# Mirroring the block triangle of a two-layer graph kernel, and storing turned dilation decisions for the second layer

## The chip, the cores and the metric

The kernel runs on one core of a Trainium2 chip. A core has five engines that run at the same time, each through its own queue of instructions in order: TensorE (PE in the profile, its weight loads PEld), VectorE (DVE), ScalarE (ACT), GpSimd (POOL) and SyncE (SP). SP and POOL also issue DMA transfers, which 16 DMA engines carry out. The metric is the device time of one execution in microseconds (us), the median of several runs.

## The reference

The input is 16 graphs of N = 1024 nodes with 128 features, and a dense weighted adjacency matrix for each graph whose pattern of non-zeros is symmetric while its values are not.

```python
# layer 0: three convolutions, each
h = h @ W + b
nh = h / max(norm(h), EPS)
ew = adj * (nh @ nh.T)          # the cosine matrix is symmetric, adj is not
h = ew @ h                      # relu between them
x = x + h

# layer 1
keep = dilate(adj > 0)          # row by row, each removal clears its mirror too
adj_d = adj * keep
for i in (1, 2, 3):
    agg = (adj_d @ x) / clip(adj_d.sum(-1), 1)
    out = agg @ Wr + x @ Wx + b
    h_i = batchnorm(relu(out / max(norm(out), NORM_EPS)))
x = x + concat(h_1, h_2, h_3) @ Wl + bl
```

The dilation is sequential: row n counts its neighbours, and if there are more than ten it removes those whose running rank divides evenly by half the count; what row n removes is also removed from column n, before the next row is looked at.

## The kernel before, in words

The adjacency of a graph is 8 x 8 blocks of 128 x 128. The kernel works on block rows q of the upper triangle with the diagonal: row q holds the blocks (q, q) to (q, 7), and beside them their mirror images from below the diagonal, so that one tile of `2 * (8 - q) - 1` blocks carries both. Row 0 is the longest, row 7 the shortest.

Layer 0 (class `Batch`) goes through the rows in the order of `SEQ`, a long one and a short one in turn. For a row, `products` makes the cosine blocks once by matmul and multiplies them into both halves of the tile (the diagonal block by an instruction of its own); `turn` transposes the mirror half on PE; `sums` and `sums_back` add up the result. `adjT_tile` loads the adjacency of a row, transposes the blocks of one half and stores them to DRAM (`adjT_d`) for the second layer.

The dilation runs at the same time, spread between the steps of layer 0. It is cut into 16 pieces: block row k (0 to 7) by half of the graphs (8 each). At the start of a piece, `loads` fetches for each graph the adjacency rows (`an`), and the decisions that earlier rows made on these columns: the tile `pk` (named `kl`, two buffers), loaded from `keep_d` by a transposing DMA on SP's queue (L810). `rounds` solves the sequential rule inside the diagonal block, and `scans` writes the row's decisions `kp` as 0 or 1 in half precision to `keep_d`, 128 rows of 1024, through POOL's queue (L989).

The instructions of layer 0 and the dilation are put in order by the class `Plan` in the kernel itself: it simulates the five queues with prices of its own, a landing time of 3.5 us for a DMA among them, and fixes the order on every engine. The second layer after it is ordered by the framework's scheduler, which moves ready instructions ahead of those that still wait.

In the first part of the second layer ("stage First" below) the kernel takes one graph after the other. `fetch` loads all decisions of a graph (`kb`, eight loads of 128 x 1024, L407) one graph ahead. For each row q, `load_row` loads the transposed half from `adjT_d` (L396) and the plain half from the input (L398); `masked` turns the decisions of the blocks (q, q) to (7, q) on PE into PSUM (L1416), multiplies them with those of row q on DVE (L1418, an edge stays only if neither side removed it), and applies the product to both halves of the adjacency (L1424 and L1428); `turn` transposes the masked mirror half (L1441), copies it back on ACT (L1442) and stores both halves to `adT_d` (L1443 and L1445) for the later convolutions; `First.add` adds up the aggregation (L1199) two rows behind, `weigh` divides by the degree (L1221 to L1225) and `norms` normalises four blocks (L1113 on ACT, L366, L369, L1115 and L1132 on DVE). The next convolution of the graph before (`onward`, L1253 and L1261) and its transposes (`keep`, L1138) are put between the rows. The tiles of a row are used by every second graph, so that the load of a row waits until `onward` has read the tile for the last time.

Of the kernel before, what the change touches and what calls it, by code (L numbers as in the profile page):

```python
# [9 lines left out]
F32 = mybir.dt.float32  # L10
# [9 lines left out]
P = 128  # L20
# [18 lines left out]
SEQ = (0, 7, 1, 6, 2, 5, 3, 4)  # L39
# [220 lines left out]
def tile_adj_preln_d2(  # L260
# [49 lines left out]
    def base(q):  # L310


        return q * 2 * NCH - q * q
# [3 lines left out]
    adT_d = [dram.tile([NCH, P, N], F32, tag=f"adT{b}", name=f"adT{b}") for b in range(B)]  # L317
    sum_d = [[dram.tile([P, N], F32, tag=f"sum{l}_{b}", name=f"sum{l}_{b}") for b in range(B)] for l in (1, 2)]
# [64 lines left out]
    EARLY = (0, 1)  # L383
    early, kept = {}, {}

    def row_of(b, q):

        pool, tag = kept["early" if q in EARLY else "rows"], f"aT{q}"
        if b % 2:
            pool, tag = kept["rows"], f"aTo{q}"  # L390
        return pool.tile([P, 2 * (NCH - q) - 1, P], F32, tag=tag, name=f"aT{q}_{b}")

    def load_row(b, q):
        row = NCH - q
        aT = row_of(b, q)
        nc.sync.dma_start(aT[:, :row, :].rearrange("p c q -> p (c q)"), adjT_d[b][q][:, q * P :])  # L396
        if row > 1:
            nc.sync.dma_start(  # L398
                aT[:, row:, :].rearrange("p c q -> p (c q)"), adj[b][q * P : (q + 1) * P, (q + 1) * P :]
            )  # L400
        return aT

    def fetch(b):

        kb = kept["k"].tile([P, NCH, N], F16, tag="kb", bufs=2, name=f"kb_{b}")
        for c in range(NCH):
            nc.sync.dma_start(kb[:, c, :], keep_d[b][c * P : (c + 1) * P, :])  # L407
# [5 lines left out]
    with ExitStack() as actx:  # L413
# [42 lines left out]
        def adj_piece(b, q):  # L456
            Nat[b, q] = nat = poold.tile([P, NCH, P], F32, tag="nat", bufs=4, name=f"nat_{b}_{q}")
            nc.sync.dma_start(
                nat[:, : NCH - q, :], adj[b][q * P :, q * P : (q + 1) * P].rearrange("(c p) q -> p c q", p=P)
            )  # L460

        def adjT_tile(b, q):

            place, nat, row = adj_place(b, q), Nat.pop((b, q)), NCH - q
            if row > 1:
                nc.sync.dma_start(
                    place[:, row:, :].rearrange("p c q -> p (c q)"), adj[b][q * P : (q + 1) * P, (q + 1) * P :]
                )
            for c in range(0, row, CPH):
# [4 lines left out]
                nc.scalar.activation(place[:, c : c + n, :], pt[:, :n, :], AF.Copy)  # L474
            nc.gpsimd.dma_start(adjT_d[b][q][:, q * P :], place[:, :row, :].rearrange("p c q -> p (c q)"))  # L475

        class Batch:
# [65 lines left out]
            def products(self, s):  # L543
# [5 lines left out]
                row = NCH - q  # L549

                most = max(NCH - SEQ[s % 4], NCH - SEQ[s % 4 + 4])
                ew = pool1.tile([P, 2 * most - 1, P], F32, tag=f"ew{s % 4}", name=f"ew_{nm}")
                place = adj_place(self.b, q)
                both = [t[:, 1 : 2 * row - 1, :].rearrange("p (t c) q -> p t c q", t=2) for t in (ew, place)] if row > 1 else None
                for c in range(0, row, CPH):
# [5 lines left out]
                        rhs=self.nhT[:, (q + c) * P : (q + c + n) * P],  # L561
# [3 lines left out]
                    own = c == 0  # L565
                    if own:
                        nc.vector.tensor_tensor(ew[:, 0, :], pg[:, 0, :], place[:, 0, :], ALU.mult)  # L567
                    if n > own:
                        off = slice(c + own - 1, c + n - 1)
                        nc.vector.tensor_tensor(  # L570
                            both[0][:, :, off, :],
                            pg[:, own:n, :].unsqueeze(1).to_broadcast([P, 2, n - own, P]),
# [5 lines left out]
            def turn(self, s, ew):  # L578

                q = SEQ[s]  # L580
                row = NCH - q
                for c in range(1, row, CPH):
                    n = min(CPH, row - c)
                    pt = ps_t.tile([P, CPH, P], F32, tag="gt", name=f"gt_{self.b}_{self.l}_{q}_{c}")
                    at = row + c - 1
                    for i in range(n):
                        nc.tensor.transpose(pt[:, i, :], ew[:, at + i, :], ident)  # L587
                    nc.scalar.activation(ew[:, at : at + n, :], pt[:, :n, :], AF.Copy)  # L588

            def sums(self, s, ew):  # L590
# [4 lines left out]
                for h in range(q // CPH, NHALF):  # L595
                    c = max(q, h * CPH)
                    n = (h + 1) * CPH - c
# [3 lines left out]
                        rhs=ew[:, c - q : c - q + n, :].rearrange("p c q -> p (c q)"),  # L601
# [4 lines left out]
            def sums_back(self, s, ew):  # L606

                q = SEQ[s]

                closes = all(c // CPH > q // CPH for c in SEQ[s + 1 :])  # L610
                for n in range(1, NCH - q):
                    nc.tensor.matmul(  # L612
                        self.po[:, q * P : (q + 1) * P],
                        lhsT=self.hS[:, q + n, :],
                        rhs=ew[:, NCH - 1 - q + n, :],
                        start=False,
                        stop=closes and n == NCH - 1 - q,
# [35 lines left out]
        def layer0():  # L653
# [29 lines left out]
            for i, now in enumerate(order + [None]):  # L683
# [5 lines left out]
                for s in range(NCH if now else LAG):  # L689
                    q = SEQ[s]  # L690
                    if now:
                        behind.append((now, s, *now.products(s)))
                        yield (NCH - q) * COLS
                    late = None
                    if len(behind) > LAG or not now:
                        late, s_, ew = behind.pop(0)
                        late.sums(s_, ew)
                        yield (NCH - SEQ[s_]) * COLS
                    if s > 0 and now or s == 0 and i:
                        b_, *of = behind[-2 if now else -1]  # L700
                        if now or s == 0:
                            b_.turn(*of)
                            yield (NCH - 1 - SEQ[of[0]]) * TURN
                    if late:
                        late.sums_back(s_, ew)
                        yield (NCH - 1 - SEQ[s_]) * COLS
                    if not now:
                        continue
                    while pieces_at < len(pieces) and pieces[pieces_at][0] == (i, s):
# [4 lines left out]
                        yield (NCH - pieces[pieces_at - 1][1][1]) * TURN  # L714
# [63 lines left out]
        def dilate(k, half, exact):  # L778
# [20 lines left out]
            def loads():  # L799
                for i in range(BH):  # L800
# [7 lines left out]
                    if k:  # L808
# [3 lines left out]
                        )  # L812
                        nc.vector.scalar_tensor_tensor(
# [272 lines left out]
    with ExitStack() as bctx:  # L1086
# [79 lines left out]
        class First:  # L1166
# [29 lines left out]
            def add(self, q, aT):  # L1196

                def one(c, blk, source):
# [4 lines left out]
                        start=source == 0 and c % self.ga == 0,  # L1203
                        stop=c == q and source == NCH - 1 and (c == NCH - 1 or c % self.ga == self.ga - 1),
                    )

                row = NCH - q
                for c in range(q, NCH):
                    one(c, c - q, q)
                for n in range(1, row):  # L1210
                    one(q, row + n - 1, q + n)
# [459 lines left out]
```

## Time and profile before

| | |
|---|---|
| time, median of 3 runs | 2672.81 us (2667.66 to 2675.88) |
| the profiled execution | 2669.1 us, of which 2667.4 us lie between its first and last instruction |
| PE busy | 2588.9 us, 97% |
| DVE, ACT, POOL busy | 1787.9 us, 1470.4 us, 688.5 us |
| granted TensorE clock, mean | 0.993 |
| layer 0 with the dilation | 0 to about 1410 us, the rest of layer 0 to about 1530 us |
| stage First | about 1530 to 2160 us, 38.5 us for a graph in its steady part |
| later convolutions | to the end |

In the lines of the profile, a row of a group names the line, the engine, the operation, the tiles written and read, the shapes and the count; then the busy time of the group, the mean length of one instruction, and how long the engine sat idle before. Matmuls overlap: the length of one is its latency, and the distance between two starts is what it takes from PE. Single-precision matmuls (not transposes) go through PE in two passes, and each pass is a row of the trace.

### The profile page before, as it was taken

Reading aid. Unit: us, or ns where it says so; the run is one execution under the profiler, and the core shown is the slowest. Engines: PE = TensorE matmul, PEld = TensorE weight load, DVE = VectorE, ACT = ScalarE, POOL = GpSimd, SP = SyncE. Lnnn points to the kernel's source line nnn. Section 1 sums busy time; section 2 is a strip of 40 time slices with the busy share of each in tenths; the row PEclk is TensorE's granted clock in tenths of the full one; section 3 lists DMA queues with packets and bytes.
Section 4 is the critical chain, followed back from the end, with each engine's and each line's share of the span. In section 5 each row is a group of like instructions: output and inputs, shape, how many; then the busy total and the mean of one; then the engine's idle time right before and its main releaser. Section 6 shows DMA issues by size and latency. Waiting matters only on the chain. (4 is left out here: it accounts for less than half of the span.)

```text
span 2667.4 us, 48644 instructions
## 1 busy us (share of the span) xinstructions
PE 2588.9 (97%) x16761; PEld 1992.4 (75%) x16761; DVE 1787.9 (67%) x4799; ACT 1470.4 (55%) x4209; POOL 688.5 (26%) x1141
## 2 busy tenths in 40 slices
PE   8999999999999999999999999999999999999978
PEld 6777777777777777777776789889889865655678
DVE  3767778777877789788784465555546545565565
ACT  6868687577666676575563333323333335555565
POOL 4122222122221222222220132333323322222460
PEclk9999999999999999999999999999999999999999
DMA  9457386285565587584642099999999979999427
GB/s 291 142 177 225 102 253 199 64 254 176 139 211 136 166 254 169 149 258 121 177 152 101 17 307 293 319 278 291 317 276 287 278 213 377 347 348 331 155 80 222
DMA packets 400705, 576.70 MB, mean 216 GB/s; under 512 B 87809, under 2 KB 277249, under 8 KB 400449
## 3 DMA queue, kind: packets, MB, share of 16 engines
q1 hardware_dynamic: 348416, 391.72, 48.0%
q0 software_dynamic: 52032, 181.78, 22.4%
q8 instruction: 135, 2.21, 0.3%
q14 instruction: 122, 0.99, 0.1%
HBM read 369.89 MB, written 188.81 MB: 209 GB/s over the span
## 5 line engine op out<-in xcount | busy, mean ns | idle before, releaser
L558 PE MATMUL pg<-nhT 128*128 128x512 f32 (+3 forms) x1152 | 445.9, 490 | 11.1 <-DVE ew L570 7.1
L598 PE MATMUL po<-ew,hS 128*128 128x512 f32 (+3 forms) x1152 | 445.2, 491 | 6.1 <-PEq L1071 3.6
L570 DVE TENSOR_TENSOR ew<-pg,adjA 128x768 f32<-128x768 f32 (+3 forms) x528 | 430.0, 824 | 1.0 <-PE pg L558 0.8
L612 PEld LDWEIGHTS po<-ew,hS 128*128 128x128 f32 x2688 | 338.7, 192 | 39.2 <-issue 38.3
L612 PE MATMUL po<-ew,hS 128*128 128x128 f32 x2688 | 366.5, 276 | 0.0
L588 ACT ACTIVATE ew<-gt 128x512 f32<-128x512 f32 (+1 forms) x480 | 209.3, 467 | 234.3 <-PE gt L587 229.0
L535 POOL TENSOR_TENSOR hS<-hN,rn 128x128 f32<-128x128 f32 x384 | 169.3, 474 | 481.3 <-DVE rn L369 360.2
L598 PEld LDWEIGHTS po<-ew,hS 128*128 128x128 f32 x1152 | 193.8, 191 | 94.9 <-issue 62.9
L567 DVE TENSOR_TENSOR ew<-pg,adjA 128x128 f32<-128x128 f32 x384 | 108.3, 282 | 226.3 <-PE pg L558 151.2
L558 PEld LDWEIGHTS pg<-nhT 128*128 128x128 f32 x1152 | 187.2, 191 | 94.9 <-issue 65.9
L1199 PE MATMUL agg<-hw,aT 128*128 128x129 f32 x2048 | 257.8, 276 | 0.0
L1199 PEld LDWEIGHTS agg<-hw,aT 128*128 128x128 f32 x2048 | 241.2, 191 | 0.0
L587 PEld LDWEIGHTS gt<-ident,ew 128*128 128x128 f32 x1344 | 165.7, 141 | 96.9 <-issue 74.0
L1536 PE MATMUL sumb<-aT,o 128*128 128x512 f32 x512 | 225.5, 593 | 1.8 <-ACT o L1130 1.8
L587 PE MATMUL gt<-ident,ew 128*128 128x128 f32 x1344 | 208.7, 274 | 1.8 <-DVE ew L570 1.4
L1442 ACT ACTIVATE aT<-pta 128x512 f32<-128x512 f32 (+3 forms) x160 | 71.2, 467 | 205.9 <-PE pta L1441 194.1
L1536 PEld LDWEIGHTS sumb<-aT,o 128*128 128x128 f32 x512 | 94.6, 190 | 109.2 <-issue 99.2
L532 ACT ACTIVATE hS<-hN 128x128 f32<-128x128 f32 x384 | 114.6, 302 | 77.6 <-DVE hN L516 62.7
L475 POOL DMA_DIRECT2D adjT<-adjA x128 | 70.6, 552 | 335.6 <-ACT adjA L474 295.8
L1418 DVE TENSOR_TENSOR both<-pkb,kb 128x1024 f16<-128x1024 f16 (+7 forms) x128 | 57.6, 450 | 147.7 <-PE pkb L1416 128.9
L1253 PE MATMUL next<-aT,o 128*128 128x512 f32 (+3 forms) x384 | 151.1, 497 | 0.0
L974 ACT ACTIVATE kp<-rank,fin 128x1024 f16<-128x1024 uint8 x128 | 146.7, 1150 | 6.7 <-DMA keep<-kp 5.1
(213 smaller groups left out, 5054.5 us busy)
## 6 DMA issues: line engine op xcount, KB each, us to landing
an<-in_adj_dram SPq DMA_DIRECT2D x128, 512.0 KB, 5.0
aT<-adT SPq DMA_DIRECT2D x128, 512.0 KB, 8.9
keep<-kp POOLq DMA_DIRECT2D x128, 256.0 KB
kb<-keep SPq DMA_DIRECT2D x128, 256.0 KB, 6.5
sum<-sum POOLq DMA_DIRECT2D x64, 256.0 KB
A<-sum SPq DMA_DIRECT2D x32, 512.0 KB, 4.1
xb<-in_x_dram SPq DMA_DIRECT2D x31, 512.0 KB, 4.6
adT<-aT POOLq DMA_DIRECT2D x32, 448.0 KB
```

The costliest lines, as they stand in the source:

```text
L532: nc.scalar.activation(hS[:, c, :], self.hN[:, c, :], AF.Square, accum_out=ss[:, c : c + 1])
L535: nc.gpsimd.tensor_tensor(hS[:, c, :], self.hN[:, c, :], self.rn[:, c : c + 1].to_broadcast([P, D]), ALU.mult)
L558: nc.tensor.matmul(pg[:, :n, :].rearrange("p c q -> p (c q)"), lhsT=self.nhT[:, q * P : (q + 1) * P], rhs=self.nhT[:, (q + c) * P : (q + c ...
L570: nc.vector.tensor_tensor(both[0][:, :, off, :], pg[:, own:n, :].unsqueeze(1).to_broadcast([P, 2, n - own, P]), both[1][:, :, off, :], ALU ...
L587: nc.tensor.transpose(pt[:, i, :], ew[:, at + i, :], ident)
L588: nc.scalar.activation(ew[:, at : at + n, :], pt[:, :n, :], AF.Copy)
L598: nc.tensor.matmul(self.po[:, c * P : (c + n) * P], lhsT=self.hS[:, q, :], rhs=ew[:, c - q : c - q + n, :].rearrange("p c q -> p (c q)"), ...
L612: nc.tensor.matmul(self.po[:, q * P : (q + 1) * P], lhsT=self.hS[:, q + n, :], rhs=ew[:, NCH - 1 - q + n, :], start=False, stop=closes and ...
L974: nc.scalar.activation(kp, rank if exact else rank.bitcast(U8).rearrange("p (c l) -> p c l", l=2)[:, :, i % 2], AF.Abs, bias=shift[:, i : ...
L1199: nc.tensor.matmul(self.place(c), lhsT=aT[:, blk, :], rhs=self.hw[:, source, :], start=source == 0 and c % self.ga == 0, stop=c == q and s ...
L1253: nc.tensor.matmul(self.bank[:, (c - h * CPH) * P :], lhsT=self.o[:, q, :], rhs=aT[:, c - q : hi - q, :].rearrange("p c q -> p (c q)"), st ...
L1536: nc.tensor.matmul(banks[h], lhsT=now.o[:, q, :], rhs=aT[:, h * HALF : (h + 1) * HALF], start=q == 0, stop=q == NCH - 1,)
```

## The change

The triangle is mirrored: a row q now holds the blocks (q, 0) to (q, q), so that row 7 is the longest, and all loops over rows, sources and halves run the other way round. In a tile the plain half now comes first and the turned half with the diagonal block behind it. In `products` the diagonal block lies at the end of a row, not at its beginning.

In the dilation, the decisions that a transposing DMA has loaded for block row k (the blocks above the diagonal, turned) are now also stored, through POOL's queue, to a new DRAM tensor `keepT_d`. In the second layer `fetch` loads for each row q the plain decisions of the blocks (q, 0) to (q, q) and the turned ones of the blocks (0, q) to (q-1, q), by 15 loads in place of 8, the bytes being the same. `masked` turns only the diagonal block on PE, and multiplies the others from the two loaded halves on DVE.

```diff
-SEQ = (0, 7, 1, 6, 2, 5, 3, 4)
+SEQ = (7, 0, 6, 1, 5, 2, 4, 3)
...
     def base(q):
-        return q * 2 * NCH - q * q
+        return q * q
...
+    keepT_d = [dram.tile([N, N], F16, tag=f"keepT{b}", name=f"keepT{b}") for b in range(B)]
...
-    EARLY = (0, 1)
+    EARLY = (7, 6)
...
     def load_row(b, q):
-        row = NCH - q
         aT = row_of(b, q)
-        nc.sync.dma_start(aT[:, :row, :].rearrange("p c q -> p (c q)"), adjT_d[b][q][:, q * P :])
-        if row > 1:
-            nc.sync.dma_start(
-                aT[:, row:, :].rearrange("p c q -> p (c q)"), adj[b][q * P : (q + 1) * P, (q + 1) * P :]
-            )
+        nc.sync.dma_start(aT[:, q:, :].rearrange("p c q -> p (c q)"), adjT_d[b][q][:, : (q + 1) * P])
+        if q:
+            nc.sync.dma_start(aT[:, :q, :].rearrange("p c q -> p (c q)"), adj[b][q * P : (q + 1) * P, : q * P])
         return aT

     def fetch(b):
-        kb = kept["k"].tile([P, NCH, N], F16, tag="kb", bufs=2, name=f"kb_{b}")
-        for c in range(NCH):
-            nc.sync.dma_start(kb[:, c, :], keep_d[b][c * P : (c + 1) * P, :])
+        kb = kept["k"].tile([P, base(NCH), P], F16, tag="kb", bufs=2, name=f"kb_{b}")
+        for q in reversed(range(NCH)):
+            rows = slice(q * P, (q + 1) * P)
+            for of, lo, n in ((keep_d, base(q) + q, q + 1), (keepT_d, base(q), q)):
+                if n:
+                    nc.sync.dma_start(kb[:, lo : lo + n, :].rearrange("p c q -> p (c q)"), of[b][rows, : n * P])
...
             def products(self, s):
...
-                    own = c == 0
+                    own = c + n == row
                     if own:
-                        nc.vector.tensor_tensor(ew[:, 0, :], pg[:, 0, :], place[:, 0, :], ALU.mult)
+                        nc.vector.tensor_tensor(ew[:, 2 * q, :], pg[:, n - 1, :], place[:, 2 * q, :], ALU.mult)
                     if n > own:
-                        off = slice(c + own - 1, c + n - 1)
+                        off = slice(c, c + n - own)
...
                         nc.sync.dma_start(
                             pk[:, :k, :].rearrange("p j q -> p (j q)"), keep_d[b][: k * P, cols], transpose=True
                         )
+                        nc.gpsimd.dma_start(keepT_d[b][cols, : k * P], pk[:, :k, :].rearrange("p j q -> p (j q)"))
...
             def masked(b, q, kb):
-                row = NCH - q
...
-                pk = ps_t.tile([P, NCH, P], F16, tag="pk", name=f"pkb_{b}_{q}")
-                for c in range(row):
-                    nc.tensor.transpose(pk[:, c, :], kb[:, q + c, q * P : (q + 1) * P], ident16)
+                k0 = base(q)
+                own = kb[:, k0 + 2 * q, :]
+                pk = ps_t.tile([P, P], F16, tag="pk", name=f"pkb_{b}_{q}")
+                nc.tensor.transpose(pk, own, ident16)
                 both = poolk.tile([P, NCH, P], F16, tag="both", bufs=2, name=f"both_{b}_{q}")
-                nc.vector.tensor_tensor(
-                    both[:, :row, :],
-                    pk[:, :row, :],
-                    kb[:, q, q * P :].rearrange("p (c q) -> p c q", q=P),
-                    ALU.mult,
-                )
-                nc.vector.scalar_tensor_tensor(
-                    aT[:, :row, :], aT[:, :row, :], 0.0, both[:, :row, :], ALU.max, ALU.mult
-                )
-                if row > 1:
-                    nc.vector.scalar_tensor_tensor(
-                        aT[:, row:, :], aT[:, row:, :], 0.0, both[:, 1:row, :], ALU.max, ALU.mult
-                    )
+                nc.vector.tensor_tensor(both[:, q, :], pk, own, ALU.mult)
+                if q:
+                    nc.vector.tensor_tensor(
+                        both[:, :q, :], kb[:, k0 : k0 + q, :], kb[:, k0 + q : k0 + 2 * q, :], ALU.mult
+                    )
+                    nc.vector.scalar_tensor_tensor(aT[:, :q, :], aT[:, :q, :], 0.0, both[:, :q, :], ALU.max, ALU.mult)
+                nc.vector.scalar_tensor_tensor(
+                    aT[:, q:, :], aT[:, q:, :], 0.0, both[:, : q + 1, :], ALU.max, ALU.mult
+                )
                 return aT
...
                 if len(behind) > LAG1: ...
-                if q == CPH + 1:
-                    s.norms(0)
-                if q == NCH - 1:
-                    s.norms(1)
+                if q == CPH - 1:
+                    s.norms(1)
+                if q == 0:
+                    s.norms(0)
...
-                for q in range(NCH):
+                for r in range(NCH):
+                    q = NCH - 1 - r
...
-                        was.onward(0, 0, 1)
+                        was.onward(1, 7, 6)
```

In `weigh`, banks of three block columns are closed from the end: the columns 6 and 7 first, then 3 to 5, then 0 to 2. `adjT_tile`, `turn`, `sums`, `sums_back`, `First.add` and `onward` change only in the direction of their indices.

## The prediction

> **What bounds the kernel now.** I read the table by stages first: stretches of 100 us, with the busy time of PE (count), PEld, DVE, ACT and POOL, the granted clock, the DMA share and GB/s. The first row lies in layer 0, the second in stage First.
>
> ```profile
> 600.00:700.00 100.00, 97.70 (x626) 71.96 (x625) 83.66 (x213) 66.82 (x175) 20.66 (x39) 1.00 0.41 123
> ...
> 1700.00:1800.00 100.00, 99.84 (x763) 87.73 (x763) 51.92 (x150) 29.47 (x96) 29.45 (x47) 1.00 0.99 283
> ```
>
> PE is full in both, at the full granted clock. In First the DMA share of 0.99 looks like a second bound, so I read the DMA next: one graph of First (it begins at 1800.03 with its first mask transpose) in stretches of 2 us, and the waits of SP's queue in First (who, for whom, us in total, times, longest).
>
> ```profile
> 1800.00:1802.00 2.00, 1.92 (x13) 1.58 (x12) 0.00 (x0) 1.21 (x3) 0.54 (x1) 1.00 1.06 402
> ...
> 1810.00:1812.00 2.00, 2.00 (x20) 1.96 (x19) 2.00 (x7) 1.09 (x5) 2.00 (x3) 1.00 1.05 397
> ...
> 1818.00:1820.00 2.00, 2.00 (x21) 2.00 (x20) 1.26 (x5) 0.00 (x0) 1.30 (x2) 1.00 0.96 24
> ```
>
> ```profile
> SPq L396 <- PE next L1253: 224.2, 12, 20.5
> SPq L398 <- DMA hN<-h: 17.3, 13, 1.4
> ```
>
> The loads are a burst: at about 400 GB/s for some 18 us, then 24 GB/s with SP waiting up to 20.5 us per graph until PE has read the old row tiles. The transfers thus follow PE; DMA is not the bound over a graph, but it is full in the first half. There the DVE is full too (2.00 of 2.00 at 1810). Last I read the lines that the change takes away, and how they lie on PE.
>
> ```profile
> L1416 PE MATMUL pkb<-ident,kb 128*128 128x128 f16 x576 | 55.5, 219 | 0.0
> ```
>
> ```profile
> 1805.22 0.55 PE L1416 MATMUL pkb<-ident,kb 128*128 128x128 f16 x7
> 1805.61 1.08 PE L1253 MATMUL next<-aT,o 128*128 128x512 f32 x2
> ...
> 1808.68 0.50 PE L1416 MATMUL pkb<-ident,kb 128*128 128x128 f16 x6
> 1809.02 1.35 PE L1199 MATMUL agg<-hw,aT 128*128 128x129 f32 x10
> 1810.21 0.88 PE L1441 MATMUL pta<-ident,aT 128*128 128x128 f32 x6
> ```
>
> One transpose is 219 ns long, but seven in a row let the next matmul start after 1805.61 - 1805.22 = 0.39 us, six after 0.34: each takes 0.056 us from PE. The group's 55.5 us (0.096 us each) counts tails that overlap the next work.
>
> **The change, part by part.** The sum is made against the profiled execution, 2669.1 us, 3.7 us below the median of 2672.8.
>
> *Removed on PE.* Of 576 mask transposes the 16 x 8 = 128 diagonal ones stay, 448 go: 448 x 0.056 = 25.1 us, or 28 x 0.056 = 1.57 us for a graph, in a stage where PE has no gap that would swallow it. The Trainium skill would price them higher: "TensorE: Matmul & The Clock Gate", Part 4: PE-mode transpose, gives about 275 ns for a 16-bit one inside a kernel; 448 of these would be an estimated 123 us. The spacing in the trace decides, since the transposes here are issued back to back.
>
> *DVE in First.* L1418 (616 ns for 7 blocks, 225 for one) becomes one multiply of the diagonal block and one of the others, from SBUF. No row shows this with both inputs from loaded tiles except L944, 688 ns for 1024 elements against 692 for L1418 of that size, so I take the same rate: 0.2 us more a row. DVE is at 52%, and the multiply of the other blocks no longer waits for PE.
>
> *What is late next.* The order of the changed program tells. Times from the graph's first mask transpose (1800.03 now). PE: `pw` starts at 0.46 as now and takes 3.46, two aggregations (four passes of 0.112) and a mask transpose end at 4.43, seven `pta` at 0.109 at 5.20, an aggregation and a mask transpose at 5.48, six `pta` at 6.14, then 30 passes, a mask transpose and 22 passes: PE reaches the `pta` of the third row (q = 5) at 12.0. DVE must have masked that row. Its steps (lengths less 0.08 us, by which the timeline shows them to overlap): the fourth bias add ends at 4.99 (ACT hands it over at 4.6, as now); diagonal mask 0.15, masks of row 5 0.38, row 6 of 896 elements 1.01, degrees 0.22, diagonal mask 0.15: 6.9. Now the last three blocks of the graph before are divided (first done at 7.25), ACT squares four blocks at 0.43 to 9.1, root, reciprocal and mask end at 9.95, four scalings of 0.195 at 10.73, and only behind these stand the two masks of row 5 (0.87 and 0.82): 12.42. In the kernel before, the scheduler puts those masks between these small steps. PE waits 0.5 us here, and by the same count 0.2 us at row 4 (needed at 14.0, ready at 14.2). Now the two waits are 0.1 us together. Net 0.6 us for each of 15 graphs (the first has none before it): 9 us. Bounds: 0, if the lengths hide a little better; 1.5 us a graph, if row 5's second load lands 1 us later than I count, which takes back nearly all of the gain.
>
> *The loads of First.* On SP the seven additional `kb` issues stand ahead of hN and of rows 5 to 0. Eight loads are under way at a time; SP's issues wait for the landing of the eighth before. Now eight `kb` issues take 6.33 us, 2.1 MB at 331 GB/s: bytes set this, and they stay the same. Fifteen issues at the 0.37 us spacing that unhindered loads show take 5.6 us. So I count 0 to 0.5 us for the landing of row 5, whose loads (now row 2's) end some 10 us after the first mask transpose and are wanted at 10.7 and 11.6. The upper bound, 15 times the present 0.79 us, would be 5.5 us later. The Trainium skill speaks against this part: "DMA: Bandwidth & Descriptors", Rules for kernel authors, has it that below 64 KB a transfer is mostly overhead and small ones should be joined; four of the fifteen loads are 64 KB or less, and the page's fixed 2 us each, if not overlapped, would be an estimated 8 us a graph. With eight under way the row of 6.33 us shows overlap.
>
> *The stores in the dilation.* 112 stores on POOL (552 ns per issue in L989: 62 us on an engine busy 26%), 14.7 MB more in a stage that moves 120 to 250 GB/s. Each stands in POOL's queue behind the landing of a `kl` load; behind it wait `keep` stores, `adjT` stores and the `hS` scaling. `hS` is wanted five rows later, 20 us (48 passes of eight rows in 1500 us, 3.9 us a row). The load holds its buffer until the store has landed, and SP's queue (`an`, `nat`, `xb`) stands behind the next `kl`. The view of the tile `kl` (idle time of DVE before its use, us and times; then the landing of its loads):
>
> ```profile
>   DMA kl<-keep: 0.5, 2
> ...
> DMA to landing us min/median/max: 2.2/4.3/8.2
> ```
>
> DVE waited for `kl` only twice, 0.5 us in all. The landing of a POOL store is not in the page; by the `kl` loads' 2.2 to 8.2 us, a buffer is held 3 to 9 us longer. Two buffers and 14 bursts of eight loads in 20 to 30 us bear about 4 us a load; at the upper end each burst stretches by several us. The kernel's own planner counts the store with its 3.5 us, and in the order it fixes, the dilation's matmuls stand at the same share of layer 0's columns as before, within 0.2%. I take +2 us, bounds 0 and +40.
>
> *Layer 0.* The mirror keeps every PE shape. Rows of five blocks lose one of three DVE multiplies: 945 + 411 becomes 1211 ns, 48 times 0.145 = 7 us of DVE, where DVE is at 84% and PE at 98%. PE's waits there for DVE at `pg` are a few us; I take -1, bounds -6 and +6 for the changed interleaving.
>
> *The end of First.* The last closing bank has three columns in place of two, and the last half to be normalised is the first that `keep` reads: at most +1 us once; taken as 0.
>
> Sum: -25 + 9 + 2 - 1 = -15 us: 2654 in the profiled execution, 2658 as a median.
>
> **The rivals.**
>
> A, *DVE keeps up:* the waits for row 5 stay at today's 0.1 us a graph. For it: the scheduler that made the order filled today's PE to within 0.1 us. Against: the normalisation ahead of both masks. Time: 2672.8 - 25 + 1 = 2649.
>
> B, *the gain is swallowed in First:* row 5 lands late or the chain is longer, 1.5 us a graph, DMA at 400 GB/s being what sets the first half. Against: 8 us at 24 GB/s later in the graph. Time: 2672.8 - 25 + 22 + 1 = 2671.
>
> C, *slower: the held `kl` buffers stop the dilation.* Place: L810 on SP, then L813 on DVE, whose fixed order holds layer 0's multiplies behind it, and PE behind these. Price: 0.3 us that reaches PE for each of 112 loads is 34 us: 2672.8 - 16 + 34 = 2691. It decides from 16 / 112 = 0.14 us a load. For it: SP already waits 0.4 ms in layer 0 at L810 for DVE to release the buffers. Against: 0.5 us of DVE waits for `kl`, and POOL idle three quarters of the time.
>
> **How the numbers follow.** Forecast (2649 to 2665) 0.50; A and below 0.12; B (2665 to 2681) 0.18; C, or a still longer chain, above 2681, 0.20. A measurement of this kernel can tell about 0.3%, 8 us, from no change: faster below 2664.8, 0.62; within 0.18; slower 0.20. The range leaves out a little of A and half of C: 2645 to 2690. The forecast alone would be 2649 to 2665.
>
> **What would show it.** Mask transposes x128 at 219 ns. A graph of First takes 38.5 - 1.0 = 37.5 us. PE waits for DVE's masks of rows 5 and 4 in each graph, before the `pta` of these rows. `kb` loads x240 with SP waiting less long for PE, DMA near 400 GB/s for as long as now. In layer 0, up to 1410 us, the same times to within 3 us and next to no DVE wait for `kl`. I am wrong if DVE or SP waits for `kl` by tens of us, if the part before First is longer by over 8 us, or if a graph of First doesn't shrink.

## The result, and the profile after

The changed kernel takes 2817.81 us (median; 2813.0 to 2819.56), against 2672.76 us before: 1.054 times as long, 95% interval 1.052 to 1.056. The forecast was 2658. The profiled execution spans 2815.9 us against 2667.4, 148.5 us more. The first and the last mask transpose on PE (`pkb`) cut the span into three parts:

| us | before | after | difference |
|---|---|---|---|
| up to the first mask transpose: layer 0, dilation | 1533.9 | 1526.7 | -7.2 |
| first to last mask transpose: stage First | 612.1 | 774.1 | +162.0 |
| from there to the end | 521.4 | 515.1 | -6.3 |

The whole loss lies in stage First, where one graph (from one issue of the degree store to the next, mean of eleven) takes 51.4 us in place of 39.4. (I had taken 38.5 for the steady part before; the steady period is 39.4.) Layer 0 and the rest are no longer than before. Here are the stretches of 100 us of the changed kernel; columns: busy time and count of PE, PEld, DVE, ACT and POOL, granted clock, DMA share, GB/s.

```profile
600.00:700.00 100.00, 97.98 (x628) 72.55 (x627) 82.90 (x208) 66.32 (x175) 25.27 (x47) 1.00 0.44 131
...
1700.00:1800.00 100.00, 78.44 (x552) 69.29 (x551) 45.06 (x134) 25.09 (x75) 24.13 (x38) 0.88 0.83 231
```

Layer 0 is as it was. In First PE has fallen from 99.84 to 78.44, all other engines with it, and DMA from 283 to 231 GB/s: nobody is full. So something waits, and the waits of 1700 to 2000 us of the changed kernel (us in total, times, longest) say on what. First PE, then DVE:

```profile
PE pta L1432 <- DVE invdeg L1219: 38.1, 4, 10.4
PE pta L1432 <- DVE aT L1419: 29.8, 6, 12.3
```

```profile
DVE aT L1419 <- DMA aT<-in_adj_dram: 55.5, 17, 10.3
...
DVE aT L1420 <- DMA aT<-adjT: 23.5, 7, 9.1
```

PE waits ahead of the transposes of masked rows (`pta`), for DVE; DVE waits to mask a row (L1419, L1420), for the landing of that row's loads. In the kernel before PE had no wait in these 300 us. The issues and landings by size (KB, median us to landing) show which rows are late:

```profile
aT<-adjT SPq DMA_DIRECT2D x16, 384.0 KB, 5.8
aT<-adjT SPq DMA_DIRECT2D x16, 320.0 KB, 14.6
aT<-adjT SPq DMA_DIRECT2D x16, 256.0 KB, 17.5
```

The third-longest row lands 5.8 us after its issue, the next two need 14.6 and 17.5 us. A transfer of 256 KB takes under 1 us at 400 GB/s, so I looked at one graph in steps of 2 us, with the same columns. The changed kernel:

```profile
1814.00:1816.00 2.00, 2.00 (x20) 2.00 (x20) 1.37 (x6) 1.70 (x9) 2.00 (x3) 1.00 1.09 291
...
1820.00:1822.00 2.00, 0.04 (x1) 0.04 (x1) 1.78 (x4) 0.00 (x0) 0.53 (x1) 1.00 2.18 203
1822.00:1824.00 2.00, 2.00 (x12) 2.00 (x13) 0.31 (x2) 0.77 (x2) 0.04 (x1) 0.61 0.44 29
1824.00:1826.00 2.00, 0.68 (x4) 0.31 (x2) 0.00 (x0) 0.60 (x1) 0.00 (x0) 0.50 1.03 86
1826.00:1828.00 2.00, 0.00 (x0) 0.00 (x0) 0.00 (x0) 0.00 (x0) 0.00 (x0) 0.50 0.83 118
1828.00:1830.00 2.00, 0.00 (x0) 0.00 (x0) 0.00 (x0) 0.00 (x0) 0.00 (x0) 0.50 0.98 215
...
1834.00:1836.00 2.00, 2.00 (x11) 2.00 (x10) 2.00 (x5) 0.60 (x1) 1.27 (x2) 0.50 0.78 269
1836.00:1838.00 2.00, 2.00 (x20) 2.00 (x19) 0.57 (x2) 0.00 (x0) 0.78 (x2) 0.97 0.79 241
...
1842.00:1844.00 2.00, 2.00 (x21) 1.99 (x20) 1.02 (x4) 0.49 (x1) 0.16 (x1) 1.00 0.00 0
```

From 1822 to 1828 the DMA engines move 29 to 118 GB/s, and yet their share of busy time is 0.44 to 1.03: they are occupied, and move next to nothing. The last line shows what an idle DMA looks like: share 0.00 at 0 GB/s. PE stands still meanwhile. The kernel before, in the graph that the prediction shows, has the same stretch:

```profile
1816.00:1818.00 2.00, 2.00 (x23) 1.99 (x21) 1.19 (x3) 1.20 (x2) 0.64 (x2) 1.00 1.95 191
...
1820.00:1822.00 2.00, 2.00 (x17) 1.74 (x16) 1.55 (x5) 1.69 (x7) 0.00 (x0) 1.00 0.76 23
1822.00:1824.00 2.00, 2.00 (x21) 1.99 (x20) 0.00 (x0) 0.00 (x0) 0.00 (x0) 1.00 0.79 72
```

There PE works through it. In both kernels the stretch begins some 5 to 7 us after one instruction: POOL's store of the inverse degrees (`rd`, L1234 before, L1232 after), 4 KB that the program stores as 1,024 single elements (the neighbours in a partition lie 512 bytes apart in DRAM). The trace records each such store as 16 packets of 256 bytes; before they start 4.9 to 6.0 us after the issue in this graph, after 4.6 to 6.3 us. Each is over in 0.08 us, but packets of other transfers that start just behind them take up to 6.8 us before and 5.8 after. What differs is which loads are still outstanding at that moment. The order of time of SP's queue before (start, length, line, transfer, count); the store is issued at 1811.12, when the last row load is out:

```profile
1794.88 4.97 SPq L407 DMA_DIRECT2D kb<-keep  x8
1800.74 0.38 SPq L409 DMA_DIRECT2D hN<-h  x1
1801.29 0.82 SPq L396 DMA_DIRECT2D aT<-adjT  x1
...
1810.79 0.32 SPq L396 DMA_DIRECT2D aT<-adjT  x1
```

After, the store is issued at 1814.70, and most row loads stand behind it:

```profile
1799.22 0.32 SPq L396 DMA_DIRECT2D aT<-adjT  x1
...
1803.03 0.33 SPq L408 DMA_DIRECT2D kb<-keep  x1
...
1812.46 0.38 SPq L410 DMA_DIRECT2D hN<-h  x1
1813.00 1.77 SPq L396 DMA_DIRECT2D aT<-adjT  x1
1814.82 0.42 SPq L398 DMA_DIRECT2D aT<-in_adj_dram  x1
...
1822.50 1.10 SPq L398 DMA_DIRECT2D aT<-in_adj_dram  x1
1831.15 0.32 SPq L396 DMA_DIRECT2D aT<-adjT  x1
```

Over eleven graphs (medians): from the first row load of a graph to the load of its third row it is 10.0 us before and 13.8 us after; from that first load to the degree store 19.1 us before and 15.5 after. So the loads come 3.8 us later and the store 3.6 us earlier. Of a graph's 15 row loads, 0.6 are issued within 15 us behind the store before, 7.3 after (means).

### The profile page after: what moved, and what is told of

Its sections match the earlier page's. It is cut to its first block, busy times and chain, and to the rows that moved or that the text cites. A ratio compares the mean times of both kernels' runs of the same rounds, so it can differ in the third digit from the quotient of the medians.

```text
span 2815.9 us, 48348 instructions
## 1 busy us (share of the span) xinstructions
PE 2590.0 (92%) x16313; PEld 1996.6 (71%) x16313; DVE 1795.6 (64%) x4863; ACT 1476.9 (52%) x4209; POOL 750.3 (27%) x1253
## 5 line engine op out<-in xcount | busy, mean ns | idle before, releaser
L571 DVE TENSOR_TENSOR ew<-pg,adjA 128x1024 f32<-128x1024 f32 (+1 forms) x480 | 428.6, 893 | 161.7 <-PE pg L559 119.0
L1198 PE MATMUL agg<-hw,aT 128*128 128x129 f32 x2048 | 275.5, 289 | 0.1
L1198 PEld LDWEIGHTS agg<-hw,aT 128*128 128x128 f32 x2048 | 263.8, 206 | 1.9 <-issue 0.5
L1432 PE MATMUL pta<-ident,aT 128*128 128x128 f32 x448 | 77.0, 299 | 150.8 <-DVE invdeg L1219 89.6
L1432 PEld LDWEIGHTS pta<-ident,aT 128*128 128x128 f32 x448 | 53.5, 153 | 168.1 <-issue 97.7
L1436 POOL DMA_DIRECT2D adT<-aT x112 | 88.2, 788 | 264.0 <-ACT aT L1433 246.4
L1419 DVE SCALAR_TENSOR_TENSOR aT<-aT,both 128x896 f32<-128x896 f32 (+6 forms) x112 | 77.0, 688 | 125.9 <-DMA aT<-in_adj_dram 121.3
```

The lines of the kernel that those rows point to most:

```text
L571: nc.vector.tensor_tensor(both[0][:, :, off, :], pg[:, : n - own, :].unsqueeze(1).to_broadcast([P, 2, n - own, P]), both[1][:, :, off, :], ...
L1198: nc.tensor.matmul(self.place(c), lhsT=aT[:, blk, :], rhs=self.hw[:, source, :], start=source == NCH - 1 and c % self.ga == 0, stop=c == q ...
L1432: nc.tensor.transpose(pt[:, i, :], aT[:, c + i, :], ident)
L1436: nc.gpsimd.dma_start(adT_d[b][:q, :, q * P : (q + 1) * P].rearrange("n p t -> p n t"), aT[:, :q, :])
```

## The experiments

Theory 1: the degree store stalls the DMA engines, and the change put the row loads behind it. Theory 2: 15 block loads in place of 8 delay the rows by themselves. Theory 3: VectorE's order (normalisation ahead of the masks), as forecast, only dearer. The results, as median time and, in brackets, the period of a graph in First from the trace:

| order, block loads | degrees stored as 1,024 elements | as 8 rows of 512 bytes |
|---|---|---|
| before, 8 loads ahead of the rows | 2673 (39.4) | 2659 (39.3) |
| before, 15 loads ahead | 2796 (48.5) | 2683 (40.8) |
| before, 8 loads behind | 2671 (39.4) | not run |
| after, 15 loads ahead | 2818 (51.4) | 2694 (42.9) |
| after, 15 loads behind | 2642 (38.9) | 2624 (37.6) |

The runs were made on several chips, on which the kernel before took 2667 to 2685 us. So a small difference between two of these times counts only by the ratios to before on the same chip, which stand with each run, or by the traces.

**The degree store as rows, in the changed kernel.**

```diff
-nc.gpsimd.dma_start(rd_d[b].rearrange("o (c p) -> p (o c)", p=P), invdeg[:, b, :])
+pr = ps_sm.tile([P, P], F32, tag="sm", name=f"pr_{b}")
+nc.tensor.transpose(pr[:NCH, :], invdeg[:, b, :], ident)
+rr = poolw.tile([P, HALF], F32, tag="sum", bufs=2, name=f"rr_{b}")
+nc.scalar.activation(rr[:NCH, :P], pr[:NCH, :], AF.Copy)
+nc.gpsimd.dma_start(rd_d[b].rearrange("o (c p) -> (o c) p", p=P), rr[:NCH, :P])
```

> The changed kernel, with one edit: the store of the inverse degrees (1,024 single elements of 4 bytes a graph) is turned on TensorE first and stored as 8 rows of 512 bytes. Theory 1 (the degree store stalls the DMA engines for some 8 to 10 us, and the row loads of rows 5 to 0 now stand behind it): the row loads land as in the kernel before, the period of a graph falls from 51 to 37.5-39 us, 12 to 13 us by 16 graphs less 2 to 5 us for the added transposes, so 2620 to 2690 us. Theory 2 (15 block loads in place of 8, ahead of the rows, hold the rows back by themselves): 2780 to 2820 us. Theory 3 (VectorE has the normalisation ahead of the masks, as forecast, only dearer): 2800 to 2820 us.

Measured: 2694.44 us, 1.0054 of before [1.0031, 1.0076]. 123 of the 145 us are back, though not the full gain that theory 1 promised: a graph takes 42.9 us, not 37.5 to 39. The steps of 2 us of this kernel, where the store is issued at 1811.9:

```profile
1816.00:1818.00 2.00, 0.96 (x9) 0.77 (x7) 2.00 (x6) 0.00 (x0) 0.61 (x1) 1.00 1.07 433
1818.00:1820.00 2.00, 1.53 (x12) 1.33 (x12) 0.38 (x2) 1.12 (x3) 0.00 (x0) 1.00 0.98 380
1820.00:1822.00 2.00, 0.00 (x0) 0.00 (x0) 1.26 (x4) 0.14 (x1) 1.13 (x2) 1.00 1.08 422
```

The stretch of 20 to 120 GB/s is gone, and the two late rows land after 8.0 and 9.8 us. PE still waits (0.96, 1.53, 0.00): the rows are late even without the stall. Theories 2 and 3 asked for 2780 us or more; as the main cause they are out.

**The block loads behind the row loads.**

```diff
-                    if r == 1 and b + 1 < B:
+                    if r == 6 and b + 1 < B:
                         then = fetch(b + 1)
```

> The changed kernel, with the block loads of the next graph asked for ahead of that graph's seventh row in place of its second, so that they stand behind nearly all row loads in SyncE's queue. Theory 1 (degree store): the row loads are issued 8 to 10 us earlier in the graph, most of them land before the store is issued, and most of the 145 us comes back: 2660 to 2720 us. Theory 2 (the 15 loads themselves): the same, 2660 to 2720 us. Theory 3 (VectorE's order): 2800 to 2820 us, since the masks' order is not touched.

Measured: 2641.62 us, 0.9856 of before [0.9817, 0.9896], better than either theory asked, and faster than the kernel before. The store with its elements is still there, and so is the stall; in this graph it is issued at 1835.7:

```profile
1840.00:1842.00 2.00, 2.00 (x21) 1.99 (x21) 1.93 (x8) 0.00 (x0) 0.49 (x1) 1.00 2.21 253
1842.00:1844.00 2.00, 2.00 (x21) 2.00 (x20) 1.96 (x6) 1.10 (x2) 1.29 (x3) 1.00 0.94 35
1844.00:1846.00 2.00, 2.00 (x15) 1.59 (x14) 0.60 (x2) 0.59 (x1) 0.17 (x1) 1.00 0.36 33
```

33 to 35 GB/s, and PE at 2.00 of 2.00: now block loads stand in it, which are wanted a graph later.

Against theory 3 this run says less than I expected of it, because the scheduler also changed VectorE's order. In the changed kernel the four scalings of the normalisation (L1131) stand ahead of both masks of the third row, as the prediction had it; here both masks stand ahead of them. The lines of the changed kernel (start, length, line, idle time and what ended it) and then those of this run:

```profile
1817.14 0.88 DVE L1131 TENSOR_SCALAR o<-o,rn 128x128 f32<-128x128 f32 x4
1820.21 0.96 DVE L1420 SCALAR_TENSOR_TENSOR aT<-aT,both 128x768 f32<-128x768 f32 x1 [2.20 <-DMA aT<-adjT]
1821.09 0.82 DVE L1419 SCALAR_TENSOR_TENSOR aT<-aT,both 128x640 f32<-128x640 f32 x1
...
1831.20 0.83 DVE L1420 SCALAR_TENSOR_TENSOR aT<-aT,both 128x640 f32<-128x640 f32 x1 [8.89 <-DMA aT<-adjT]
```

```profile
1835.98 0.81 DVE L1419 SCALAR_TENSOR_TENSOR aT<-aT,both 128x640 f32<-128x640 f32 x1
1836.71 0.95 DVE L1420 SCALAR_TENSOR_TENSOR aT<-aT,both 128x768 f32<-128x768 f32 x1
...
1839.23 0.87 DVE L1131 TENSOR_SCALAR o<-o,rn 128x128 f32<-128x128 f32 x4
```

But the first lines show what holds the changed kernel: VectorE is done with the normalisation and sits idle 2.20 us until the third row has landed, and 8.89 us until the next has. The order does not make this loss.

**The degree store twice.** The changed kernel stores the degrees a second time, to a scratch tensor.

```diff
 nc.gpsimd.dma_start(rd_d[b].rearrange("o (c p) -> p (o c)", p=P), invdeg[:, b, :])
+nc.gpsimd.dma_start(rd2_d[b].rearrange("o (c p) -> p (o c)", p=P), invdeg[:, b, :])
```

> The changed kernel, with the store of the inverse degrees made a second time, into a scratch that nobody reads: only the count of these 4 KB stores differs. Theory 1: a second stall of 8 to 10 us behind the first in every graph, with row loads still outstanding: 100 to 160 us more, 2910 to 2980 us. Theories 2 and 3: 64 KB more to move in all, 0 to 10 us more, 2815 to 2830 us.

Measured: 2814.19 us, 1.052 of before [1.0471, 1.0568], no slower than the changed kernel. My theory foretold 100 to 160 us more, and that was wrong. The second store is issued 0.9 us behind the first and lands with it (16.8 and 16.1 us after their issues in the graph at 1958 us). In another graph of this run the store is issued at 1851.1:

```profile
1856.00:1858.00 2.00, 1.51 (x14) 1.48 (x14) 0.84 (x3) 0.77 (x2) 0.56 (x1) 1.00 2.64 293
1858.00:1860.00 2.00, 0.20 (x3) 0.00 (x0) 0.00 (x0) 0.60 (x1) 0.00 (x0) 1.00 1.50 19
...
1864.00:1866.00 2.00, 0.00 (x0) 0.00 (x0) 0.00 (x0) 0.00 (x0) 0.00 (x0) 0.50 0.77 79
1866.00:1868.00 2.00, 0.00 (x0) 0.00 (x0) 0.83 (x1) 0.00 (x0) 0.63 (x2) 0.50 0.96 231
```

Over eleven graphs the stretch under 150 GB/s is 9.0 us long (median), against 7.5 us with one store. So its length is not a price per element that adds up; two such stores at one time share one stall. Why is open.

**The kernel before, with its block loads in 15 pieces.** The same bytes; seven of the eight loads are cut in halves.

```diff
-nc.sync.dma_start(kb[:, c, :], keep_d[b][c * P : (c + 1) * P, :])
+for h in range(1 if c == NCH - 1 else 2):
+    part = slice(0, N) if c == NCH - 1 else slice(h * HALF, (h + 1) * HALF)
+    nc.sync.dma_start(kb[:, c, part], keep_d[b][c * P : (c + 1) * P, part])
```

> The kernel before, with the same bytes of the decisions loaded in 15 pieces of 128x512 and 128x1024 in place of 8 of 128x1024 (seven rows of blocks in halves). Theory 1: the row loads are issued 3 to 6 us later, the last one or two rows fall behind the degree store: 2 to 8 us a graph, 2700 to 2800 us. Theory 2 (the count of loads is the cost): 9 us a graph, 2800 to 2820 us. Theory 3 (the order on VectorE is the cost): 2665 to 2680 us, as before.

Measured: 2795.72 us, 1.0436 of before [1.0374, 1.0498]. This cut of the loads alone, without any other part of the change, costs nearly as much as the change as a whole. It lies at the edge between the two theories' ranges; in the trace the load of the third row comes 13.2 us after the first (10.0 before), and 3.1 row loads are issued behind the degree store in place of 0.6. VectorE's order is here, step by step, that of the kernel before, so theory 3 has no part in this loss. The next run decides between the other two.

**The same, with the degrees stored as rows** (both edits above on the kernel before).

> The kernel before, with its block loads in 15 pieces (which alone gave 2796 us) and the inverse degrees stored as 8 rows of 512 bytes. Theory 1 (the 15 loads cost time because they push the last row loads behind the degree store): without that store's stall about 100 of the 116 us come back, 2685 to 2715 us. Theory 2 (15 loads in place of 8 cost it by themselves): 2780 to 2810 us.

Measured: 2682.70 us, 1.0002 of before [0.9983, 1.0021]: against before on the same chip the loss is gone. The same stretch of 100 us, first with the elements, then with rows:

```profile
1600.00:1700.00 100.00, 80.97 (x592) 73.51 (x591) 43.22 (x119) 24.09 (x76) 22.24 (x35) 0.90 0.85 228
```

```profile
1600.00:1700.00 100.00, 97.26 (x753) 86.22 (x752) 56.84 (x152) 32.74 (x104) 27.83 (x45) 1.00 0.86 295
```

Fifteen loads cost 1.5 us a graph by themselves here (39.3 to 40.8), and 9.1 when they push row loads behind the store (39.4 to 48.5). The cost is the meeting of the two.

**Both repairs in the changed kernel.**

> The changed kernel with both repairs: block loads behind the row loads, and the inverse degrees stored as 8 rows of 512 bytes. If with the late block loads only loads with slack stand in the stall (theory 1), the second repair adds nothing and its 16 transposes cost 5 us at most: 2636 to 2652 us, against 2642 us with the late block loads alone. Rival: the stall still holds something in the path, 3 us a graph or more: 2590 to 2625 us.

Measured: 2624.43 us, 0.979 of before [0.9772, 0.9807], the fastest kernel of the study. The time lies in the rival's range, though the price is not the rival's 3 us: even with late block loads the stall still cost 1.3 us a graph (38.9 to 37.6). Another 9 us lie between the last degree store and the end of the program (516.3 to 507.3 us); how far that part can be trusted is said below, with the degrees as rows in the kernel before. Now nothing holds PE:

```profile
1700.00:1800.00 100.00, 100.00 (x746) 89.31 (x745) 63.56 (x187) 34.48 (x105) 31.76 (x52) 1.00 0.91 326
```

In 1700 to 2000 us this kernel's PE shows no wait at all. DVE has the same work as in the changed kernel, but both masks of the third row again stand ahead of the scalings.

**The kernel before, with late block loads** (`if q == 1` becomes `if q == 6`).

> The kernel before, with its block loads moved behind the row loads in the same way. If the row loads already came in time there (theory 1), the move is worth nothing without the change: 2660 to 2685 us, and the 31 us by which the changed kernel with late block loads beats the kernel before are the change's own. Rival: the move is worth the 31 us by itself: 2630 to 2655 us.

Measured: 2671.45 us, 0.996 of before [0.9945, 0.9975], and the period of a graph unchanged at 39.4 us. The move repairs what the change broke; it is worth at most a small part of the gain by itself.

**The kernel before, with the degrees as rows.**

> The kernel before, with the inverse degrees stored as 8 rows of 512 bytes. Theory 1: the stall is there in the kernel before too, but the row loads are ahead of it, so its removal brings nothing: 2668 to 2682 us, with the added transposes at up to 5 us. If it falls by more than 10 us, the kernel before was already paying for the stall.

Measured: 2659.00 us, 0.9974 of before [0.9964, 0.9985], a little below the range given; before took 2666.6 us on this chip. The period stays (39.3), as theory 1 says. The two profiled executions differ by 11 us behind the last degree store (517.9 to 506.4 us). This part scatters: it is 511.1 to 517.9 us in the nine profiled executions with elements and 506.4 to 511.1 in the five with rows, and in the changed kernel 511.1 with either. Rows are some 6 us shorter there in the mean; that the last stall is the reason was not shown.

**The transposes put back**, with late block loads, and then with both repairs.

```diff
-pk = ps_t.tile([P, P], F16, tag="pk", name=f"pkb_{b}_{q}")
+pka = ps_t.tile([P, NCH, P], F16, tag="pk", name=f"pkb_{b}_{q}")
+for c in range(q):
+    nc.tensor.transpose(pka[:, c, :], kb[:, k0 + c, :], ident16)
+pk = pka[:, q, :]
```

> The changed kernel with late block loads (2642 us), and the 448 transposes of off-diagonal decision blocks put back on TensorE; nobody reads what they turn, and the masks still come from the stored transposes. It prices the forecast's largest term, 448 by 0.056 us. If TensorE is the bound of the stage again: 20 to 30 us more, 2662 to 2672 us. Rival (TensorE has slack in the stage, or the transposes lie in its idle time): 2640 to 2650 us.

> The changed kernel with both repairs (2624 us, a kernel whose TensorE waits for nothing in this stage), and the 448 transposes of off-diagonal decision blocks put back on TensorE, read by nobody. With late block loads alone their price came out at 12 us, where TensorE still waited for other things. If they cost what the forecast's term says (448 by 0.056 us, 25.1 us) wherever TensorE is the bound: 2645 to 2653 us, and a graph of 39.2 us in place of 37.6. Rival (they are cheaper than the spacing of the row before shows, 12 us also here): 2634 to 2639 us.

Measured: 2653.24 us (0.9895 of before [0.9878, 0.9913]) against 2641.62, and 2649.89 us (0.9944 [0.9927, 0.9961]) against 2624.43. That is 12 us where PE still had gaps (it was busy 96.44 of 100 us from 1700 to 1800), and 25.5 us where it had none. These last two kernels ran on different chips (before took 2681 and 2667 us there), so I go by their traces: the period of a graph goes from 37.6 to 39.3 us, and the whole stage First from 585.3 to 610.9 us, 25.6 us more.

**The stores of the dilation alone, on the kernel before.**

```diff
+keepT_d = [dram.tile([N, N], F16, tag=f"keepT{b}", name=f"keepT{b}") for b in range(B)]
...
+nc.gpsimd.dma_start(keepT_d[b][cols, : k * P], pk[:, :k, :].rearrange("p j q -> p (j q)"))
```

> The kernel before, with the 128 stores of the turned decisions added in the dilation and nothing else; nobody reads them. It prices the forecast's term for these stores (2 us, bounds 0 to 40). By the forecast: 2670 to 2682 us. Rival C of the prediction (the stores hold the kl buffers and stop the dilation, at 0.14 us a load or more): 2690 us or more.

Measured: 2670.59 us, 1.0013 of before [0.9995, 1.003].

**The degree store from ScalarE's queue, in the changed kernel** (`nc.gpsimd` becomes `nc.scalar` in that one line).

> The changed kernel, with the same store of 1,024 single elements issued by ScalarE in place of GpSimd (the same bytes, the same pieces of 4 bytes, another queue). If the pieces of 4 bytes make the stall, whoever issues them: 2780 to 2830 us, with the same stretch of 20 to 110 GB/s from 6 us behind the issue. Rival (GpSimd's queue makes it): the stretch is gone and the time is near that of the store in rows, 2690 to 2715 us.

Measured: 2806.18 us, 1.045 of before [1.0417, 1.0483], a graph of 50.4 us. The stretch is there (the store is issued at 1809.2), so the small pieces make it, not GpSimd's queue (the trace records 1,024 packets of 4 bytes for each store here):

```profile
1813.00:1815.00 2.00, 1.65 (x15) 1.46 (x14) 0.13 (x1) 0.00 (x0) 0.00 (x0) 1.00 1.42 87
1815.00:1817.00 2.00, 0.00 (x0) 0.00 (x0) 0.00 (x0) 0.00 (x0) 0.00 (x0) 1.00 0.78 101
```

## Why the prediction was wrong, point by point

**The step that failed is the reading of the slow stretch.** The prediction said that the loads are a burst at 400 GB/s, "then 24 GB/s with SP waiting up to 20.5 us per graph until PE has read the old row tiles", and that "DMA is not the bound over a graph". It took the stretch for slack. The line itself, 1818 to 1820 us, said otherwise: share 0.96 at 24 GB/s is an occupied DMA, not an idle one. SP's wait for PE was real but lay beside it. With slack there, a few us of delay cost nothing; with the stall there, they cost the stall. The sum had no term for it; it measured 8.5 us a graph, as follows.

**The loads of First** were taken as 0 to 0.5 us later, with 5.5 us as the bound. Measured: the third row's load comes 3.8 us later. Within the bound, but the price was taken to be the delay. By themselves 15 loads cost 1.5 us a graph in the kernel before. In the changed kernel the delay, with the store 3.6 us earlier, moved 7.3 row loads behind the store, and a graph lost 8.5 us to the stall (51.4 against 42.9 with rows) and 5.3 to the position of the loads (42.9 against 37.6): 13.8 in all. The prediction's spacing of 0.37 us an issue did not hold either: from the first block load to the load of hN behind them it is 9.4 us after (1803.03 to 1812.46) and 5.9 before (1794.88 to 1800.74), or 0.5 us for each additional issue. Eight loads are under way at a time (the load issued at 1805.40 waited until the one issued eight before it, at 1799.58, had landed), and smaller ones do not land much sooner: in the changed kernel 256 KB take 4.8 us (median), 128 KB 4.7 and 5.1, 32 KB 3.3 and 3.8. The Trainium skill's rule that the prediction set aside ("DMA: Bandwidth & Descriptors", Rules for kernel authors: join small transfers) had the direction right; the 8 us a graph estimated from it was over the 3.8 us by which the row loads came later (the page fits its 2 us to transfers issued by GpSimd, and these are issued by SP). Why the position costs 5.3 us in the changed kernel and 15 loads only 1.5 in the one before was not settled. With rows the third row is issued 2.0 us ahead of the degree store in the one and 6.5 in the other, so PE is that much further on when it comes. And VectorE's order differs too: of the third row's masks one stands behind the scalings in the changed kernel with rows, none with both repairs, so the 5.3 us hold what that order costs, if anything.

**Where the 13.8 us are.** PE is busy 77% of 1600 to 2100 us, so some 11.8 of the 51.4 us of a graph are idle. The other 2.0 us I put down to the clock: in the graph shown it falls to 0.50 at 1822.5, after PE was idle from 1819.6 to 1822.0, and PE, at work again from 1833.4, has it back only at 1836.1. About 5 us of a graph's work run at half the clock, which by estimate costs half of that. The Trainium skill has a rule for this in "TensorE: Matmul & The Clock Gate", Part 1: The HAM clock gate: half rate after an idle window of some 3.4 us, full rate after one of work. This trace agrees roughly: 2.4 us without work were enough for the fall, and 2.7 us of work for the rise.

**Removed on PE**, 25.1 us: right. Put back where PE is the bound, the 448 transposes cost 25.6 us of stage First, 0.057 us each; the spacing in the trace was the price, not the 275 ns of "TensorE: Matmul & The Clock Gate", Part 4: PE-mode transpose, in the Trainium skill. The row for the 128 that stay is as foretold but for a few tails:

```profile
L1412 PE MATMUL pkb<-ident,kb 128*128 128x128 f16 x128 | 28.6, 224 | 6.0 <-DVE both L1414 6.0
```

**What is late next**, +9 us for VectorE's order: not measured. The order was as forecast in the changed kernel, but there the row loads came so late that DVE waited for them behind the normalisation. With both repairs PE waits for nothing, as rival A had it, but there the scheduler had put the masks of the third row ahead of the normalisation, so the wait that was forecast could not show.

**The stores in the dilation**, +2 us: right, no measurable time (1.0013), and rival C falls. In the changed kernel POOL waits 131.6 us for `kl` to land before it stores, and SP 69.2 us for the stores, but the one engine whose wait would count hardly waits:

```profile
DVE patt L812 <- DMA kl<-keep: 4.9, 4, 2.2
```

**Layer 0** was forecast at -1 (bounds -6 and +6); stage First begins 7.2 us earlier, in the other runs of changed kernels 6 to 10, a little outside the bounds. Which part of the mirror gives it was not tried. **The end of First**, taken as 0: the part behind the last mask transpose is 6.3 us shorter (521.4 to 515.1), but with the same code there it took 515.0 us in the run with the added stores, so this is scatter as far as can be told.

**The rivals.** B named the right place, "row 5 lands late", and priced it at 1.5 us a graph, where the loss against before is 12.0. None of the three had the degree store, which stood in no list because the change doesn't touch it. The prediction's own signs told it at once: a graph of First did not shrink.

## What to carry to other kernels

A stretch with a high DMA share and few GB/s was a stall here, not slack: find the transfer that starts it before moving loads by a few us. Work out for a change not only how late a load will be, but which slow transfer it will then stand behind, also where the change touches neither of them. And store small per-row results in rows: turned on PE, 512 bytes at a time, this one cost nothing that could be seen, and a load that is not wanted until the next graph belongs behind those that are.

## What the runs showed of the hardware that was not expected

A store of 4 KB in 1,024 elements of 4 bytes holds the other transfers of the core: 4 to 7 us after its issue they fall to some 20 to 130 GB/s, for 6.5 to 9 us in eleven graphs of the changed kernel (counted under 150 GB/s). Row loads of 128 KB to 320 KB that stand in it land after 14 to 18 us, against 8 to 10 us with the store in rows, and the store itself after 15.7 us. It does so from GpSimd's and from ScalarE's queue alike; as 8 rows of 512 bytes it does not. The Trainium skill bears on this in "DMA: Bandwidth & Descriptors", Specifications and Rules for kernel authors: full rate from 512 bytes, and one descriptor per element where the last dimension is strided. That the loads of another queue stand meanwhile, these runs show. A second such store, 0.9 us behind the first, makes the stall 1.5 us longer (7.5 to 9.0) and the kernel no slower (2814 us against 2818).
